# Graph layer on one core: attention columns copied by VectorE, SiLU on ScalarE, four groups gathered ahead

## The chip, the cores and the metric

The kernel runs on one core of one Trainium2 chip. The metric is the device time of one execution in microseconds, as a median over several executions; lower is better. The engines are called by the profile's names: PE (TensorE), DVE (VectorE), ACT (ScalarE), POOL (GpSimd) and SP (SyncE, which issues most DMAs).

## The reference

A graph layer with attention over 12,500 nodes of 64 features and 412,500 edges, sorted by receiver (`dst`); `src` is random.

```python
h = jnp.maximum(_layernorm(x, axis=-1), 0.0)
msg_in = jnp.concatenate([h[src], h[dst], edge_attr_32], axis=-1)
messages = swish(msg_in @ W1 + b1) @ W2 + b2
att = softmax(swish(msg_in @ Wa1 + ba1) @ Wa2 + ba2, axis=0)   # over all edges
agg = segment_sum(messages * att, dst)
out = x + swish(concat([h, agg]) @ Wu1 + bu1) @ Wu2 + bu2
```

## The kernel before, in words

**The head.** Nodes are padded to 12,544 and worked in seven chunks: layer norm on DVE and ACT, a transpose on PE into `hT` (features by nodes, kept in SBUF), then two tables in DRAM: `ts_d`, one row of 128 numbers per node for its part as sender, and `tr_d`, the same as receiver. All weights of the first products are halved, so that a SiLU is made as (tanh(y) + 1) y with y half the argument.

**The groups.** The edges lie in 403 groups of K = 8 tiles of 128 edges. `one_pass` is one unrolled loop over the groups g; `pin` keeps the written order on each engine. For each group:

- `load(g)`, two groups ahead: POOL gathers the sender rows from `ts_d` by one indirect DMA for each tile (L513) into a buffer `gs` of a pool of seven; SP loads receiver windows of `tr_d` into `wins`; DVE makes a 0/1 matrix `eo` (L538); PE multiplies both into the PSUM tile `pe` (L542), which holds the receiver and edge parts of 1,024 edges.
- `begin(g)`: DVE adds the gathered rows to `pe` (L553), ACT takes the tanh (L556).
- `end(g)`: DVE makes the messages (L566), the attention activation (L572), multiplies by `Wa2` (L574) and reduces to logits (L577).
- `weigh(s)`, once for each batch of four groups: the running maximum (L603, L604, L606), two exponentials on ACT (L607, L610).
- `by_node(g)`, four to five groups later: DVE makes for each of the eight tiles a matrix `wt` of weight where receiver equals column (L620), PE multiplies it with the messages (L626), ACT copies the sum (L632), PE projects it (L637), and `put(g)` adds it to the node table `sums` (L651, L655) and notes the maximum in `stand` (L658), at columns held in registers.

**Columns.** For every second group from 8 on (`picks`, 192 groups, one tile each) no row is gathered for the eighth tile. Instead ACT copies the 128 senders' columns of `hT` one by one into a tile `cols` (L483: 128 partitions by 4 bytes, the column in a register), DVE blanks the wrong half (L547), and PE multiplies with the sender weights into `pe` (L548). `spots` holds the columns' places; a register load (L479, `TENSOR_LOAD` in the trace) puts 32 of them at a time into ACT's registers, before 32 copies (`columns`, `burst`). Register loads for `put` and for the windows are at L498.

**The tail.** After the last group the node update runs in 13 tiles on all engines.

Of the kernel before, what the change touches and what calls it, by code (L numbers as in the profile page):

```python
# [39 lines left out]
PHASE = 0  # L40
FIRST = 8
SLOTS = (((0, 32), (32, 32)), ((64, 32), (96, 32)))
HT_AT = 4224
ROUND = 12582912.0
WIDE = 128
EPS = 1e-5
# [11 lines left out]
def gnn_kernel(ctx: ExitStack, tc: tile.TileContext, n_edges, x, src, src_row, dst, dst_row, first, edge,  # L58
# [73 lines left out]
    with tc.tile_pool(name="node1", bufs=1) as node1, \  # L132
# [3 lines left out]

        sizes = [8] + [min(CB, NB - 16 - c) for c in range(0, NB - 16, CB)] + [8] if NB > 16 else [NB]
# [38 lines left out]
        pin(nc.scalar.activation(node1.tile([P, 1], F32, name="spare"), eps, AF.Sqrt))  # L176
        xms, sqs, rstds, hs, tss = ({} for _ in range(5))
# [5 lines left out]
        def subtract(i):  # L183

            n = chunks[i][1]
            total = node.tile([P, CB], F32, name="total")[:, :n]
            pin(nc.vector.tensor_reduce(total, xcs[i], AX.X, ALU.add))
            xm = xms[i] = node.tile([P, CB, D], F32, name="xm", bufs=3)[:, :n, :]
            pin(nc.vector.scalar_tensor_tensor(xm, total[:, :, None].to_broadcast([P, n, D]), -1.0 / D,
                                               xcs[i], op0=ALU.mult, op1=ALU.add))  # L190

        def square(i):
            n = chunks[i][1]
            sq = sqs[i] = node.tile([P, CB, D], F32, name="sq", bufs=3)[:, :n, :]
            pin(nc.scalar.activation(sq, xms[i], AF.Square))

        def totals(i):
            n = chunks[i][1]
            rstd = rstds[i] = node.tile([P, CB], F32, name="rstd")[:, :n]
            pin(nc.vector.tensor_reduce(rstd, sqs.pop(i), AX.X, ALU.add))  # L200
# [4 lines left out]
        def normal(i):  # L205
            n = chunks[i][1]
# [37 lines left out]
        nch = len(chunks)  # L244
# [22 lines left out]
        for c, nn in chunks:  # L267
# [9 lines left out]
            pin(nc.sync.dma_start(  # L277
                tr_d[:NP, :].rearrange("(p b) f -> p b f", b=NB)[:, c:c + nn, :], tr))
        pin(nc.sync.dma_start(tr_d[NP:, :], zero[:WR, :]))
# [80 lines left out]
def one_pass(tc, n_edges, v):  # L360
# [17 lines left out]
    with ExitStack() as ctx:  # L378
# [43 lines left out]
        with tc.tile_pool(name="work2", bufs=2) as work2, \  # L422
                tc.tile_pool(name="small", bufs=3) as small, \
                tc.tile_pool(name="pre_ps", bufs=AHEAD + 1, space=PSUM) as pre_ps, \
                tc.tile_pool(name="one_ps", bufs=1, space=PSUM) as one_ps:
            pes, gss, lgs, ps_, psums, sps, pps, ees, mts, nums, cols = ({} for _ in range(11))
# [12 lines left out]
            chosen = {g: i for i, g in enumerate(picks)}  # L439
            hT8 = v["hT"].rearrange("d b p -> d (b p)").bitcast(U8)  # L440
            sets = [(i, min(P, len(picks) - i)) for i in range(0, len(picks), P)]
# [3 lines left out]
            def places():  # L445
# [4 lines left out]
                for k, (i, n) in enumerate(sets):  # L450
                    e = (picks[i] * K + K - 1) * EP
                    nc.sync.dma_start(num[:n, k, :], bass.AP(
                        tensor=v["src_row"].tensor, offset=v["src_row"][:, e:].offset,
                        ap=[[EVERY * K * EP, n], [1, EP]]))
# [8 lines left out]
                for k, (i, n) in enumerate(sets):  # L463
                    nc.sync.dma_start(par_d[k * P:k * P + n, :], low[:n, k, :])
# [3 lines left out]
            def numbers(g):  # L468
                if g in chosen:
                    n = nums[g] = small.tile([P, EP], I32, name="half", bufs=3)  # L470
                    row = par_d[chosen[g]:chosen[g] + 1, :]
                    nc.sync.dma_start(n, bass.AP(tensor=row.tensor, offset=row.offset, ap=[[0, P], [1, EP]]))
                    cols[g] = small.tile([P, EP], F32, name="cols", bufs=3)

            def columns(g, first, n):
                if g not in chosen:
                    return
                to, i = cols[g].bitcast(U8), chosen[g]
                _, regs = nc.values_load_multi_w_load_instructions(  # L479
                    spots[i % P:i % P + 1, i // P, first:first + n], engines=[ENG.Activation],  # L480
                    min_val=HT_AT, max_val=HT_AT + 2 * NP - 4, skip_runtime_bounds_check_because=WHY)
                for i in range(n):
                    pin(nc.scalar.copy(to[:, 4 * (first + i):4 * (first + i) + 4],  # L483
                                       hT8[:, bass.ds(regs[i] - HT_AT, 4)]))

            def burst(g, k):
# [6 lines left out]
            tr_w = bass.AP(tensor=tr_d.tensor, offset=tr_d.offset,  # L493
                           ap=[[C, NP + WR - SHIFT], [SHIFT * C, 2], [1, C]])

            def registers(g, engine, at, base=base_sb, top=NP - 1):
                n = min(NQ, NG + (base is not base_sb) - g)
# [6 lines left out]
            def load(g):  # L504

                t = g * K
                if g % NQ == 0:
                    registers(g, ENG.SP, at_sp)
                full = gather.tile([P, K, C], F32, name="gs")
                gs = gss[g] = full[:EP]  # L510
                for j in range(K - (g in chosen)):
# [21 lines left out]
                for r in range(2):  # L533
                    nc.sync.dma_start(win[r * R:(r + 1) * R, :, r, :],
                                      tr_w[bass.ds(at_sp[g], R), :, :])
# [14 lines left out]
            def begin(g):  # L550

                n = K - (g in chosen)
                pin(nc.vector.tensor_tensor(gss[g][:, :n, :], pes[g][:, :n, :], gss[g][:, :n, :], ALU.add))  # L553
                if n < K:
                    pin(nc.vector.tensor_copy(gss[g][:, n, :], pes[g][:, n, :]))
                pin(nc.scalar.activation(pes[g], gss[g], AF.Tanh))  # L556

            def end(g, then=None):

                s = batch[g]  # L560
                if g == starts[s]:
                    lgs[s] = small.tile([EP, B * K], F32, name="lg")
                gs, th = gss.pop(g), pes.pop(g)

                def message():
                    pin(nc.vector.scalar_tensor_tensor(acts[g % ACTS][:, :, 0:U], th[:, :, U:C], 1.0,  # L566
                                                       gs[:, :, U:C], op0=ALU.add, op1=ALU.mult))

                if g < NG - 1:
                    message()  # L570
                att = th[:, :, 0:U]
                pin(nc.vector.scalar_tensor_tensor(att, th[:, :, 0:U], 1.0, gs[:, :, 0:U],  # L572
                                                   op0=ALU.add, op1=ALU.mult))
# [3 lines left out]
                pin(nc.vector.tensor_reduce(lgs[s][:, k:k + K], att, AX.X, ALU.add))  # L577
# [4 lines left out]
                if g == NG - 1:  # L582
                    message()

            def top(s):

                n = size[s] * K
                lg = lgs[s]
# [10 lines left out]
            def weigh(s):  # L599
# [5 lines left out]
                fall = small.tile([P, 1], F32, name="fall")  # L605
                pin(nc.vector.tensor_tensor(fall, nmax[:, s + 1:s + 2], nmax[:, s:s + 1], ALU.subtract))  # L606
# [3 lines left out]
                pin(nc.scalar.activation(p[:, :n], lgs.pop(s)[:, :n], AF.Exp, bias=nmax[:EP, s + 1:s + 2],  # L610
                                         accum_out=psum))
                psums[s] = psum

            def by_node(g):
# [4 lines left out]
                for j in range(K):  # L619
                    pin(nc.vector.tensor_scalar(wt[:, j, :], iota_w[:EP, j // H, :],  # L620
                                                dloc[:, g * K + j:g * K + j + 1],
                                                p[:, k + j:k + j + 1],
                                                op0=ALU.is_equal, op1=ALU.mult))
# [94 lines left out]
            for g in range(NG):  # L718
# [6 lines left out]
                begin(g)  # L725
                if more and g < NG - 1:
# [10 lines left out]
                if g + AHEAD < NG:  # L737
                    load(g + AHEAD)
                numbers(g + 6)
# [384 lines left out]
```

## Time and profile before

| | |
|---|---|
| median of 3 runs | 3902.49 us (3900.42 to 3908.46) |
| the profiled execution's own time | 3904.89 us |
| its span, first to last instruction | 3903.1 us |
| busy PE, DVE, ACT, POOL | 61%, 80%, 76%, 74% of the span |

A row of the grouped view reads: line, engine, operation, written tile <- read tiles, shapes, count, then busy time in us, mean of one in ns, then idle time of the engine just before these instructions and what ended it. "issue" is idle time for which the profile shows nothing that was waited for. Register loads, waits and DMA issues are work of an engine's sequencer and do not count as busy. An engine runs its instructions in order.

### The profile page before, as it was taken

How to read it: one execution, taken by the hardware profiler on the slowest of the kernel's cores; microseconds unless marked ns; L12 is line 12 of the kernel's file. 1: busy time of each engine (PE TensorE's matmuls, PEld its weight loads, DVE VectorE, ACT ScalarE, POOL GpSimd, SP SyncE). 2: the span in 40 equal slices, each digit the busy share in tenths (PEclk: the TensorE clock that was granted, in tenths of full speed). 3: DMA queues.
4: the chain of work that ended last, by engine and by line, in shares of the span. 5: the costliest groups of instructions: out<-in, count | busy, mean ns of one | idle time of the engine just before them, and what ended most of it. 6: DMA issues, size and time to landing. Idle time of an engine off the chain costs nothing. (4 is left out here: it accounts for less than half of the span.)

```text
span 3903.1 us, 72226 instructions
## 1 busy us (share of the span) xinstructions
PE 2368.6 (61%) x11368; PEld 1927.2 (49%) x11368; DVE 3115.4 (80%) x8929; ACT 2954.1 (76%) x25797; POOL 2888.6 (74%) x3057
## 2 busy tenths in 40 slices
PE   6566656666666666665665656556565565555655
PEld 5454444454445554554444545445444454444545
DVE  6888787878788888887877877778777777877887
ACT  2887777777778888887877777878877878878712
POOL 3777777777777777777777777777777777777774
PEclk8766566666666657666666666666666666666666
DMA  7433334333433333333333333333333333333343
GB/s 280 114 104 94 102 100 106 94 104 99 107 93 97 97 97 91 94 97 94 87 97 85 97 93 89 97 86 97 93 88 97 86 96 91 90 97 86 95 116 86
DMA packets 228304, 391.30 MB, mean 100 GB/s; under 512 B 72369, under 2 KB 155762, under 8 KB 214770
## 3 DMA queue, kind: packets, MB, share of 16 engines
q0 software_dynamic: 97024, 198.90, 19.5%
q1 hardware_dynamic: 130802, 187.73, 17.9%
q14 instruction: 385, 3.15, 0.3%
q8 instruction: 93, 1.52, 0.2%
HBM read 360.52 MB, written 25.82 MB: 99 GB/s over the span
## 5 line engine op out<-in xcount | busy, mean ns | idle before, releaser
L513 POOL DMA_INDIRECT gs<-ts_d,src_sb x3032 | 2871.4, 947 | 973.1 <-issue 844.2
L483 ACT COPY cols<-hT 128x4 uint8 x24576 | 2415.5, 189 | 595.2 <-issue 594.2
L542 PE MATMUL pe<-wins,eo 128*128 128x256 f32 x3224 | 1470.7, 630 | 846.4 <-DVE eo L538 619.9
L542 PEld LDWEIGHTS pe<-wins,eo 128*128 128x128 f32 x3224 | 964.4, 316 | 1145.4 <-DVE eo L538 708.6
L620 DVE TENSOR_SCALAR wt<-iota_w,dloc,p 128x40 f32<-128x40 f32 x3224 | 726.9, 323 | 1.8
L553 DVE TENSOR_TENSOR gs<-pe,gs 128x1024 f32<-128x1024 f32 (+1 forms) x403 | 467.0, 1159 | 325.7 <-DMA gs<-ts_d,src_sb 303.3
L626 PE MATMUL sp<-wt,acts 128*65 128x40 f32 x6448 | 621.9, 268 | 4.6 <-DVE wt L620 3.5
L626 PEld LDWEIGHTS sp<-wt,acts 128*65 128x65 f32 x6448 | 586.0, 183 | 11.4 <-DVE wt L620 6.2
L556 ACT ACTIVATE pe<-gs 128x1024 f32<-128x1024 f32 x403 | 410.6, 1019 | 215.9 <-DVE gs L553 125.3
L637 PEld LDWEIGHTS mt<-ss,w2u 65*128 65x128 f32 x806 | 201.7, 281 | 330.4 <-issue 291.9
L637 PE MATMUL mt<-ss,w2u 65*128 65x40 f32 x806 | 183.7, 322 | 255.5 <-DVE gm L603 221.4
L566 DVE SCALAR_TENSOR_TENSOR acts<-pe,gs 128x512 f32<-128x512 f32 x403 | 277.6, 689 | 21.6 <-ACT pe L556 12.2
L574 DVE TENSOR_TENSOR pe<-pe,w_all 128x512 f32<-128x512 f32 x403 | 281.8, 699 | 13.5
L572 DVE SCALAR_TENSOR_TENSOR pe<-pe,gs 128x512 f32<-128x512 f32 x403 | 280.3, 696 | 10.5
L596 PE MATMUL mt<-ident,mx 128*128 128x128 f32 x107 | 46.7, 437 | 396.4 <-DVE sums L655 375.9
L577 DVE TENSOR_REDUCE lg<-pe 128x8 f32<-128x512 f32 x403 | 276.7, 687 | 10.5
L538 DVE TENSOR_SCALAR eo<-dbs,bj 64x256 f32<-64x256 int32 x806 | 275.5, 371 | 9.2
L596 PEld LDWEIGHTS mt<-ident,mx 128*128 128x128 f32 x107 | 19.2, 179 | 408.3 <-issue 404.5
L658 DVE COPY stand<-nmax 64x40 f32 x806 | 159.0, 197 | 3.4 <-issue 0.3
L547 DVE SCALAR_TENSOR_TENSOR cols<-half,cols 128x128 f32<-128x128 int32 x192 | 67.1, 349 | 100.6 <-ACT cols L483 98.5
L651 DVE SCALAR_TENSOR_TENSOR sums<-sums,scale,mt 64x40 f32 x214 | 54.4, 254 | 110.9 <-PE mt L637 107.4
L548 PEld LDWEIGHTS pe<-stack,cols 128*128 128x128 f32 x384 | 121.7, 317 | 32.5
(126 smaller groups left out, 957.6 us busy)
## 6 DMA issues: line engine op xcount, KB each, us to landing
eo<-in_edge_dram SPq DMA_DIRECT2D x100, 512.0 KB
dbs<-in_dst_row_dram SPq DMA_DIRECT2D x200, 256.0 KB
gs<-ts_d,src_sb POOLq DMA_INDIRECT x3032
wins<-tr_d SPq DMA_DIRECT2D x806, 32.0 KB
half<-par_d SPq DMA_DIRECT2D x192, 64.0 KB
ts_d<-ts SPq DMA_DIRECT2D x5, 896.0 KB
tr_d<-tr SPq DMA_DIRECT2D x5, 896.0 KB
hT_d<-hT SPq DMA_DIRECT2D x7, 448.0 KB
```

The lines of the kernel that those rows point to most:

```text
L483: pin(nc.scalar.copy(to[:, 4 * (first + i):4 * (first + i) + 4], hT8[:, bass.ds(regs[i] - HT_AT, 4)]))
L513: nc.gpsimd.indirect_dma_start(out=full[:rows, j, :], out_offset=None, in_=ts_d[:, :], in_offset=bass.IndirectOffsetOnAxis(ap=src_full[:ro ...
L542: pin(nc.tensor.matmul(pe[:, 2 * q:2 * q + 2, :], eo[:, q * EP:(q + 1) * EP], win[:, q // 2, :, :], start=True, stop=q < H - 1 or g not in ...
L553: pin(nc.vector.tensor_tensor(gss[g][:, :n, :], pes[g][:, :n, :], gss[g][:, :n, :], ALU.add))
L556: pin(nc.scalar.activation(pes[g], gss[g], AF.Tanh))
L566: pin(nc.vector.scalar_tensor_tensor(acts[g % ACTS][:, :, 0:U], th[:, :, U:C], 1.0, gs[:, :, U:C], op0=ALU.add, op1=ALU.mult))
L572: pin(nc.vector.scalar_tensor_tensor(att, th[:, :, 0:U], 1.0, gs[:, :, 0:U], op0=ALU.add, op1=ALU.mult))
L574: pin(nc.vector.tensor_tensor(att, att, wa2[:EP, None, :].to_broadcast([EP, K, U]), ALU.mult))
L577: pin(nc.vector.tensor_reduce(lgs[s][:, k:k + K], att, AX.X, ALU.add))
L620: pin(nc.vector.tensor_scalar(wt[:, j, :], iota_w[:EP, j // H, :], dloc[:, g * K + j:g * K + j + 1], p[:, k + j:k + j + 1], op0=ALU.is_equ ...
L626: pin(nc.tensor.matmul(sp, acts[g % ACTS][:, j, :], wt[:, j, :], start=j == 0, stop=j == K - 1))
L637: pin(nc.tensor.matmul(pp, w2u.rearrange("s h u -> s (h u)"), sps.pop(g), start=True, stop=True))
```

## The change

- **Columns move to DVE.** `PHASE = 9` leaves `picks` empty, so ACT copies no column. `vpicks` takes three groups in eight, from 9 to 390: 144 groups, one tile each. In each of the 384 iterations from 4 to 387, `vcolumns` loads 24 registers of DVE twice (after `begin`, and ahead of `end`), and `spare_columns` issues the 24 copies that belong to each load on DVE. In the built program there are 18,432 such copies and 864 loads (96 loads are cut in two where a tile ends). `fetch`, single rows fetched by SP, is off (`ROW0 = 1000`).
- **SiLU on ACT.** `begin` adds into `pe` and ACT makes two SiLUs of 512 elements, attention part and messages; the tanh and the two products on DVE go. `gs` is free after the add.
- **Softmax without Exp.** `weigh` makes exp(x) as ((1 + t) / (1 - t)) to the 16th, t = tanh(x / 32): a tanh and a square on ACT and nine small operations on DVE.
- **`wt` in two operations** of 320 elements in place of eight of 40.
- **Four groups in the head.** Rows of `x` of the first `FILL = 4` groups' senders (32 gathers) are gathered while `ts_d` does not yet exist; the layer norm and the product follow (`filled`), between the pieces of the `tr_d` loop. `load` gathers nothing for these groups.
- SP's window addresses are counted in bytes, so that no multiplication of a register is needed.

```diff
-PHASE = 0
+PHASE = 9
+FILL = 4
+ROW0 = 1000
+VTURN = 8
+VRES = (1, 4, 6)
+VSTART = 4
+VLATER = 5
...
+        early = node1.tile([P, FILL * K], I32, name="early")
+        nc.sync.dma_start(early, src[:, :FILL * K])
+        for g in range(FILL):
+            for j in range(K):
+                nc.gpsimd.indirect_dma_start(out=xes[g][:, j, :], ..., in_=x[:, :], ...)
...
+            def vcolumns(g, part):
+                at, end = (i * EP * len(VRES) // (2 * VTURN) for i in (2 * (g - VSTART) + part, ...
+                while 0 <= at < end:
+                    t, first = vpicks[at // EP], at % EP
+                    n = min(end - at, EP - first)
...
+                    loads, regs = spots_of(t, first, n, ENG.DVE)
+                    to = cols[t].bitcast(U8)
+                    waiting.extend((to[:, 4 * (first + i):4 * (first + i) + 4], regs[i]) for i in range(n))
+                    at += n
+
+            def spare_columns(n=None):
+                for to, reg in waiting[:n]:
+                    pin(nc.vector.tensor_copy(to, hT8[:, bass.ds(reg - HT_AT, 4)]))
...
-                for j in range(K - (g in chosen)):
+                for j in range(K - (g in chosen) - (g in fetched) if g >= FILL else 0):
...
-                pin(nc.vector.tensor_tensor(gss[g][:, :n, :], pes[g][:, :n, :], gss[g][:, :n, :], ALU.add))
-                if n < K:
-                    pin(nc.vector.tensor_copy(gss[g][:, n, :], pes[g][:, n, :]))
-                pin(nc.scalar.activation(pes[g], gss[g], AF.Tanh))
+                pin(nc.vector.tensor_tensor(pe[:, :n, :], pe[:, :n, :], gs[:, :n, :], ALU.add))
+                pin(nc.scalar.activation(att, pe[:, :, 0:U], AF.Silu, scale=2.0))
+                pin(nc.scalar.activation(acts[g % ACTS][:, :, 0:U], pe[:, :, U:C], AF.Silu, scale=2.0))
...
-                    pin(nc.vector.scalar_tensor_tensor(acts[g % ACTS][:, :, 0:U], th[:, :, U:C], 1.0,
-                                                       gs[:, :, U:C], op0=ALU.add, op1=ALU.mult))
-                pin(nc.vector.scalar_tensor_tensor(att, th[:, :, 0:U], 1.0, gs[:, :, 0:U],
-                                                   op0=ALU.add, op1=ALU.mult))
...
-                pin(nc.scalar.activation(scale[:, s:s + 1], fall, AF.Exp))
+                pin(nc.scalar.activation(t, lg[:, :n + 1], AF.Tanh, bias=part, scale=1.0 / 32))
+                spare_columns()
+                pin(nc.vector.tensor_scalar(d, t, -1.0, 1.0, op0=ALU.mult, op1=ALU.add))
+                pin(nc.vector.reciprocal(d, d))
+                pin(nc.vector.scalar_tensor_tensor(t, t, 1.0, d, op0=ALU.add, op1=ALU.mult))
+                for _ in range(3):
+                    pin(nc.vector.tensor_tensor(t, t, t, ALU.mult))
...
-                for j in range(K):
-                    pin(nc.vector.tensor_scalar(wt[:, j, :], iota_w[:EP, j // H, :], ...
+                pin(nc.vector.tensor_tensor(wt.rearrange("p (r h) w -> p r h w", h=H), ..., ALU.is_equal))
+                pin(nc.vector.tensor_tensor(wt, wt, p[:, k:k + K, None].to_broadcast([EP, K, W]), ALU.mult))
...
                 begin(g)
+                vcolumns(g, 0)
...
+                spare_columns()
+                vcolumns(g, 1)
                 end(g)
...
+                spare_columns()
```

More of the change, by code (lines that the diff above doesn't have):

```diff
@@ L242, in senders, with filled @@
                     ts_d.rearrange("(p b) f -> p b f", b=NB)[:, c:c + nn, :], tss.pop(i)))
-        nch = len(chunks)
+        ready = []
+        def filled(i):
+            h = hs.pop(i)
+            pt = node_ps.tile([P, 4, P], F32, name="pt")
+            for k in range(K // 2):
+                pin(nc.tensor.transpose(pt[:, k, :], h[:, 2 * k:2 * k + 2, :], ident))
+            he = node.tile([2 * D, K // 2, P], F32, name="he")
+            pin(nc.scalar.copy(he, pt))
+            gs = gather.tile([P, K, C], F32, name="gs")
+            for b in range(0, K, 4):
+                pn = node_ps.tile([P, 4, C], F32, name="pn", bufs=4)
+                for k in range(0, 4, 2):
+                    pin(nc.tensor.matmul(pn[:, k:k + 2, :], he[:, (b + k) // 2, :],
+                                         w_pair[:, 0], start=True, stop=True))
+                pin(nc.scalar.copy(gs[:, b:b + 4, :], pn))
+            ready.append(gs)
         squares(0)
@@ L278, in gnn_kernel @@
                 tr_d[:NP, :].rearrange("(p b) f -> p b f", b=NB)[:, c:c + nn, :], tr))
+        squares(nch)
+        for i in range(FILL):
+            totals(nch + i)
+            deviation(nch + i)
+            if i + 1 < FILL:
+                subtract(nch + i + 1)
+                square(nch + i + 1)
+            if i > 0:
+                filled(nch + i - 1)
+            for c in chunks[i * nch // FILL:(i + 1) * nch // FILL]:
+                receivers(*c)
+            normal(nch + i)
+        filled(nch + FILL - 1)
         pin(nc.sync.dma_start(tr_d[NP:, :], zero[:WR, :]))
@@ L425, in one_pass @@
                 tc.tile_pool(name="one_ps", bufs=1, space=PSUM) as one_ps:
-            pes, gss, lgs, ps_, psums, sps, pps, ees, mts, nums, cols = ({} for _ in range(11))
+            pes, gss, atts, lgs, ps_, psums, sps, pps, ees, mts, nums, cols = ({} for _ in range(12))
             w2t_ps = one_ps.tile([P, 4, P], F32, name="mt")[:U, 0, :S1]
@@ L484, in columns @@
                                        hT8[:, bass.ds(regs[i] - HT_AT, 4)]))
+            waiting = []
+            def vcolumns(g, part):
+                at, end = (i * EP * len(VRES) // (2 * VTURN) for i in (2 * (g - VSTART) + part,
+                                                                        2 * (g - VSTART) + part + 1))
+                end = min(end, len(vpicks) * EP)
+                while 0 <= at < end:
+                    t, first = vpicks[at // EP], at % EP
+                    n = min(end - at, EP - first)
+                    if first == 0:
+                        cols[t] = small.tile([P, EP], F32, name="vcols", bufs=VBUFS)
+                    loads, regs = spots_of(t, first, n, ENG.DVE)
+                    for one in loads:
+                        pin(one)
+                    to = cols[t].bitcast(U8)
[4 more added lines that the diff above has]
+                    pin(nc.vector.tensor_copy(to, hT8[:, bass.ds(reg - HT_AT, 4)]))
+                waiting[:] = waiting[len(waiting) if n is None else n:]
             def burst(g, k):
@@ L488, in burst @@
                     columns(g + 3 + i, *SLOTS[EVERY - 1 - i][k])
-            at_sp, at_lo, at_hi, bus, rest = {}, {}, {}, {}, {}
[L493 to L497, printed above, removed]
+            fetched = {}
+            for i in range(NG):
+                g = ROW0 + (EP * (i + 1) - 1) // ROWS + 2
+                if g < NG - 12:
+                    fetched[g] = i
@@ new lines, in one_pass, with ask, scaled @@
+            order = list(fetched)
+            ids, lone = {}, {}
+            ts8 = ts_d.rearrange("n f -> (n f)").bitcast(U8)
+            def ask(i):
+                if i < len(order):
+                    g = order[i]
+                    e = (g * K + K - 1 - (g in chosen)) * EP
+                    ids[i] = small.tile([1, EP], I32, name="ids", bufs=2)
+                    nc.sync.dma_start(ids[i], v["src_row"][:, e:e + EP])
+            def scaled(i):
+                if i < len(order):
+                    pin(nc.vector.tensor_scalar(ids[i], ids[i], 9, None, op0=ALU.logical_shift_left))
@@ new lines, in fetch @@
+            def fetch(g):
+                at = (g - ROW0) * ROWS
+                end = min(at + ROWS, len(order) * EP)
+                if g == ROW0 - 3:
+                    ask(0)
+                if g == ROW0 - 2:
+                    scaled(0)
+                while 0 <= at < end:
+                    i, first = at // EP, at % EP
+                    n = min(end - at, EP - first)
+                    if first < ROWS:
+                        ask(i + 1)
+                    if EP // 2 <= first < EP // 2 + ROWS:
+                        scaled(i + 1)
+                    if first == 0:
+                        lone[order[i]] = small.tile([P, C], F32, name="lone", bufs=2)
+                    to = lone[order[i]]
+                    loads, regs = nc.values_load_multi_w_load_instructions(
+                        ids[i][0:1, first:first + n], engines=[ENG.SP], min_val=0, max_val=(NP - 1) * 4 * C,
+                        skip_runtime_bounds_check_because=WHY)
+                    for one in loads:
+                        pin(one)
+                    for k in range(n):
+                        pin(nc.sync.dma_start(to[first + k:first + k + 1, :].bitcast(U8),
+                                          ts8[bass.ds(regs[k], 4 * C)][None, :]))
+                    at += n
@@ new lines, in one_pass, with registers @@
+            at_sp, at_lo, at_hi, bus, rest = {}, {}, {}, {}, {}
+            row = 4 * C
+            tr8 = tr_d.bitcast(U8)
+            tr_w = bass.AP(tensor=tr8.tensor, offset=tr8.offset,
+                           ap=[[1, (NP - 1) * row + 1], [row, R], [SHIFT * row, 2], [1, row]])
+            base_by = keep.tile([1, NG + 1], I32, name="base_by")
+            nc.vector.tensor_scalar(base_by[:, :NG], base_sb[:, :NG], 9, None, op0=ALU.logical_shift_left)
+            def registers(g, engine, at, base, top):
+                n = min(NQ, NG + (base is not base_by) - g)
@@ L738, in one_pass @@
                     load(g + AHEAD)
+                fetch(g)
                 numbers(g + 6)
```

113 lines of the change are left out of this document (69 added, 44 removed).

## The prediction

> **What bounds the kernel now.** I read the busy table, the waits, the costliest groups (different shapes kept apart), and then POOL's timeline at both ends.
>
> ```profile
> PE 2368.6 (61%) x11368; PEld 1927.2 (49%) x11368; DVE 3115.4 (80%) x8929; ACT 2954.1 (76%) x25797; POOL 2888.6 (74%) x3057
> POOL gs L513 <- issue: 844.2, 2770, 0.3
> POOL gs L513 <- DMA ts_d<-ts: 49.3, 1, 49.3
> POOL gs L513 <- DMA gs<-ts_d,src_sb: 34.8, 114, 0.3
> DVE gs L553 <- DMA gs<-ts_d,src_sb: 303.3, 225, 3.9
> L513 POOL DMA_INDIRECT gs<-ts_d,src_sb x3032 | 2871.4, 947 | 973.1 <-issue 844.2 <-DMA ts_d<-ts 49.3 <-DMA gs<-ts_d,src_sb 34.8
> 51.68 1.10 POOL L513 DMA_INDIRECT gs<-ts_d,src_sb  x1 [49.29 <-DMA ts_d<-ts]
> 3845.97 0.94 POOL L513 DMA_INDIRECT gs<-ts_d,src_sb  x1 [0.30 <-issue]
> ```
>
> POOL is only 74% busy, yet after the head no wait of its gathers is longer than 0.3 us, and that gap follows every gather: 0.947 busy, 0.30 between. So POOL is full: (3846.9 - 51.7) / 3032 = 1.2517 us for one gather. The time is 51.7 until `ts_d` exists, 3795 of gathers and 56.2 of tail; 3903.1 in all, and the execution's own time is 1.8 more (3904.9), 2.4 above the median. DVE waits for gathers (303 us), not the reverse. Fewer gathers save, until another engine's group exceeds POOL's.
>
> **POOL after the change.** 192 gathers replaced by ACT's columns become 144 replaced by DVE's, and 32 move to the head: 3224 - 144 - 32 = 3048, sixteen more than 3032. The 32 take 40 us of the 49.3 in which POOL idles, so they are hidden, if their indices land like the first inputs; one small DMA ahead of those on SP costs 0 to 0.6 us. POOL alone would give 51.7 + 3048 x 1.2517 + 56.2 = 3923 us; for one group with its 7.63 gathers, 9.55 us. That is the floor. The question is DVE.
>
> **DVE, ordinary work.**
>
> ```profile
> L620 DVE TENSOR_SCALAR wt<-iota_w,dloc,p 128x40 f32<-128x40 f32 x3224 | 726.9, 323 | 1.8
> L574 DVE TENSOR_TENSOR pe<-pe,w_all 128x512 f32<-128x512 f32 x403 | 281.8, 699 | 13.5
> L572 DVE SCALAR_TENSOR_TENSOR pe<-pe,gs 128x512 f32<-128x512 f32 x403 | 280.3, 696 | 10.5
> L566 DVE SCALAR_TENSOR_TENSOR acts<-pe,gs 128x512 f32<-128x512 f32 x403 | 277.6, 689 | 21.6 <-ACT pe L556 12.2
> L553 DVE TENSOR_TENSOR gs<-pe,gs 128x1024 f32<-128x1024 f32 x211 | 258.0, 1223 | 180.4 <-DMA gs<-ts_d,src_sb 161.4 <-issue 14.9 <-PE pe L542 3.0
> L553 DVE TENSOR_TENSOR gs<-pe,gs 128x896 f32<-128x896 f32 x192 | 209.0, 1089 | 145.3 <-DMA gs<-ts_d,src_sb 141.9 <-issue 0.2
> L555 DVE COPY gs<-pe 128x128 f32<-128x128 f32 x192 | 53.9, 281 | 0.0
> L606 DVE TENSOR_TENSOR fall<-nmax 128x1 f32<-128x1 f32 x107 | 17.0, 159 | 3.7
> L589 DVE TENSOR_TENSOR lg<-lg,w_all 128x32 f32<-128x32 f32 x98 | 18.9, 193 | 3.3
> 3842.18 0.16 DVE L604 TENSOR_TENSOR nmax<-gm,nmax 128x1 f32<-128x1 f32 x1
> 3842.37 0.16 DVE L606 TENSOR_TENSOR fall<-nmax 128x1 f32<-128x1 f32 x1
> 96.00:3850.00 3754.00, 2275.16 (x10973) 1848.37 (x10972) 3012.68 (x8702) 2906.84 (x25703) 2837.77 (x2997) 0.64 0.37 96
> ```
>
> The last row is the busy time of the stretch of all groups (PE, its weight loads, DVE, ACT, POOL): DVE 3012.7. Removed: `wt` 726.9, the two products 277.6 + 280.3, the copy 53.9, `fall` 17.0: 1356. Added: two `wt` operations of 320 elements; on the line from 193 ns for 32 to 699 for 512 each takes 0.50, less the overlap of their end with what follows 0.94 for both: 403 x 0.94 = 379. And nine small operations of a softmax step, each waiting for the one before (L604 and L606 of 0.16 start 0.19 apart), so 0.22 each: 107 x 2.0 = 212. Left are 2248 / 403 = **5.58 us** a group. A step's own wait for ACT's tanh is filled by 24 copies. ACT keeps two SiLUs (at 689 to 1019 ns per 512 to 1024 elements some 1.3 us a group) and is no bound.
>
> **DVE, the copies.** 48 a group, a form DVE does not run before.
>
> ```profile
> L483 ACT COPY cols<-hT 128x4 uint8 x24576 | 2415.5, 189 | 595.2 <-issue 594.2
> 2002.42 0.18 DVE L655 TENSOR_TENSOR sums<-sums,mt 64x40 f32 x1
> 2002.52 0.17 DVE L658 COPY stand<-nmax 64x40 f32 x1
> 2004.89 3.14 ACT L483 COPY cols<-hT 128x4 uint8 x32 [0.28 <-issue]
> 2008.96 3.14 ACT L483 COPY cols<-hT 128x4 uint8 x32 [0.93 <-issue]
> ```
>
> Short operations overlap: what counts is start to start. On ACT it is (3.14 - 0.19) / 31 = 0.095 us. On DVE two operations of 40 elements, both at columns from registers, start 0.10 apart; an element takes (1223 - 1089) / 128 = 1.05 ns (the two shapes of L553), so with 4 elements 0.10 - 0.038 = 0.062. I take 0.07, near DVE's own row, and keep 0.062 to 0.095: 48 x 0.07 = **3.36 us**. [...]
>
> **DVE, the register loads.** They do not count as busy and are the hidden term.
>
> ```profile
> L479 ACTq TENSOR_LOAD <-spots x768: 1942/2008/2800, 98.4 to 3706.6; - x192
> L553 DVEq EVENT_SEMAPHORE  x1420: 21/50/3717, 92.0 to 3849.7; - x178
> L498 DVEq TENSOR_LOAD <-bases x202: 336/343/600, 142.4 to 3853.0; - x101
> L498 SPq TENSOR_LOAD <-base_sb x101: 294/301/753, 87.2 to 3774.6; - x101
> L282 DVEq TENSOR_LOAD <-wrong x1: 321/321/321, 3896.2 to 3896.2; - x1
> L556 ACT ACTIVATE pe<-gs 128x1024 f32<-128x1024 f32 x403 | 410.6, 1019 | 215.9 <-DVE gs L553 125.3 <-DVE gs L555 62.8 <-DMA gs<-ts_d,src_sb 19.5
> ACT cols L483 <- issue: 594.2, 764, 1.3
> DVE sums L651 <- PE mt L637: 107.4, 89, 1.6
> DVE bu L323 <- PE mt L314: 102.8, 25, 4.5
> ```
>
> ACT's load of 32 registers takes 2.008 us. While it runs the sequencer issues nothing; the engine only finishes what is queued. The timeline shows both cases: 0.28 idle where a tanh of 1.02 stood in the queue, 0.93 where only copies did. So 2.01 - 0.93 = 1.08 us of copies were queued, some eleven.
>
> For 24 registers on DVE: SP takes 0.30 for four, ACT 2.008 for 32, so 0.061 for each further one, and 24 need 1.52; DVE's four take 0.343, 1.14 times SP's, which makes 1.74. I take 1.65. The low end is DVE's own slope from one register (0.321) to four (0.343), 0.007 each: 0.49.
>
> In the built order one load stands behind `begin`'s add in three groups of four, behind the second `wt` operation in the fourth, and one behind the first 24 copies in every group. Queued behind it is all of DVE's next work: `put`, `eo`, and the attention product, for which PE and ACT then wait. Cover by queued copies is 11 x 0.07 = 0.8; behind the add it is the add, 1.1, and what the add's split waits leave of the copies (four of 0.05 with as much between them, 0.4). Idle for four groups: three times 0.2 behind the add, 1.2 behind `wt`, four times 0.85 behind copies, 0.3 for a load cut in two, 0.2 for the two loads of `put` (0.343 each): 5.7, or **1.43 us** a group.
>
> **The sum.** 5.58 + 3.36 + 1.43 = 10.37 us a group, above POOL's 9.55: DVE becomes the bound, and POOL waits for `gs`. DVE's chain begins with the first add:
>
> ```profile
> 96.40 1.23 DVE L553 TENSOR_TENSOR gs<-pe,gs 128x1024 f32<-128x1024 f32 x1 [2.96 <-PE pe L542]
> 3849.81 1.23 DVE L553 TENSOR_TENSOR gs<-pe,gs 128x1024 f32<-128x1024 f32 x1 [1.64 <-DMA gs<-ts_d,src_sb]
> ```
>
> In the head DVE has four layer norms more, each four operations of 512 elements (0.7) and a reciprocal: 12 us. They stand among the `tr_d` work, which partly waits for DMAs, so the add at 96.4 comes 0 to 12 later, say 8: 104. (POOL does not feel it at once: groups 0 to 3 are there and three buffers are free.) PE's and ACT's part of these groups lies in ACT's idle stretch before its first tanh. Three sets of `spots` in place of two, and one table load more in the tail, are 1 us each, within that choice. Then 384 x 10.37 = 3982; nineteen groups without copies at 8, between the 5.6 and POOL's 9.98 for eight gathers: 152; from the last add to the end 53 as now. Waits on PE that POOL's pace hid come on top: `bu` 103 in full, `sums` half of 107. Together 104 + 3982 + 152 + 53 + 156 = 4447 us span, with + 1.8 and - 2.4 much the same: **4450 us**. Hidden at no cost: the gathers saved (POOL has 0.82 us a group to spare), the shorter `wt` on PE, SP's addresses. With copies of 0.062 it falls by 147, with loads of 1.52 by 100, without the waits by 156; with loads of 1.74 it rises by 70, with copies of 0.08 by 184.
>
> **The rivals.**
>
> *Loads are cheap on DVE.* With 0.49 us all are covered by queued work. DVE needs 5.58 + 3.36 and the 0.4 of the waits on PE, 9.34 us, below 9.55, and POOL stays the bound: 3923 + 2 = 3925. For it: DVE's flat slope. Against: ACT's 2.008. 11 in 100.
>
> *Gathers get shorter and nothing slows.* The eight `wt` operations ran beside them; without, the mean of 947 falls to the usual 940, and one takes 1.245. Then 51.7 + 3048 x 1.245 + 56.2 = 3903: no slower than now. It decides only if DVE also stays under 9.5. The rows speak against much:
>
> ```profile
> 2000.89 0.94 POOL L513 DMA_INDIRECT gs<-ts_d,src_sb  x1 [0.31 <-issue]
> 2003.91 1.78 DVE L620 TENSOR_SCALAR wt<-iota_w,dloc,p 128x40 f32<-128x40 f32 x8
> 2004.64 0.95 POOL L513 DMA_INDIRECT gs<-ts_d,src_sb  x1 [0.30 <-issue]
> ```
>
> A gather inside the eight takes 0.95, one outside 0.94. 5 in 100.
>
> *The copies block POOL.* If a gather stood still while copies run (3.36 of 9.55 us, 35% of the time), its 0.94 became 1.27, and 3048 x 1.58 + 108 = 4924. By the two rows above the price is 0.01 instead of 0.33; it would decide from 0.12 on, where POOL exceeds 10.37 a group (1.36 x 7.63). 2 in 100. [...]
>
> *No load is covered.* 864 x 1.65 = 1426 us idle in place of 384 x 1.43 = 549: 5325. ACT's 0.28 against 0.93 says cover works. 2 in 100.
>
> That the columns are not made by DVE at all is excluded by the built order.
>
> **How the numbers follow.** 80 in 100 for the forecast, 4450, its own range 4060 to 4750. The whole range reaches down to the cheap loads: 3920 to 4750; outside lie the shorter gathers, blocking, no cover, and the forecast's ends, some 17 in 100. About 0.2% (8 us) is what a measurement here can tell. Of the five for shorter gathers one is for a tail shorter by a product (0.7) and half a `wt` (0.9) at each of its last groups, and so for faster. Faster 0.01, same 0.04, slower 0.95.
>
> **What would show it.** Right: POOL's gathers waiting for DVE's add, not in 0.3 us steps; DVE register loads of 24 near 1.65 us; copies of 0.07 start to start; DVE idle by "issue" of some 500 us in front of copies, products and `sums`; ACT busy below 25%. Wrong: gathers still end to end at 1.25 us in mid-span (then 3925), or loads under 1 us.

## The result, and the profile after

The changed kernel takes 4679.15 us (median of 4 runs, 4676.97 to 4682.63) against 3901.9 (3900.42 to 3908.46): ratio 1.1989, 95% interval 1.1968 to 1.201. It is slower by 777 us; 4450 was forecast, with a range of 3920 to 4750. The profiled execution's own time is 4678.03, its span 4676.3.

The page's busy line, the groups and the waits of the kernel after:

```profile
PE 2366.9 (51%) x11320; PEld 1939.5 (41%) x11320; DVE 3762.2 (80%) x24774; ACT 603.4 (13%) x1645; POOL 2982.4 (64%) x3105
L649 POOL DMA_INDIRECT gs<-ts_d,src_sb x3048 | 2928.1, 961 | 1617.3 <-issue 791.5 <-DVE pe L690 752.3 <-DVE near L517 32.1
L568 DVE COPY vcols<-hT 128x4 uint8 x18432 | 1423.3, 189 | 119.3 <-issue 118.9
L706 DVE TENSOR_TENSOR att<-att,w_all 128x512 f32<-128x512 f32 x403 | 278.8, 692 | 375.3 <-issue 374.0 <-ACT att L695 1.2
L798 DVE TENSOR_TENSOR sums<-sums,mt 64x40 f32 x592 | 114.7, 194 | 110.9 <-issue 98.4 <-PE mt L780 0.4
L766 DVE TENSOR_TENSOR wt<-wt,p 128x320 f32<-128x320 f32 x403 | 199.3, 494 | 13.9
POOL gs L649 <- DVE pe L690: 752.3, 351, 7.5
DVE bu L377 <- PE mt L368: 105.9, 25, 4.5
DVE sums L794 <- issue: 24.5, 80, 0.7
DVE pe L690 <- issue: 7.8, 33, 0.6
```

POOL, which before never waited longer than 0.3 us in mid-span, now waits 351 times for DVE's add to give a buffer back, 752 us in all. DVE is no busier by its share than before (80%), but it has become the bound: of what it waits for, little but `bu` is late in mid-span, for 106 us in all, much as before. The rest of its idle time is mostly put down to "issue", in front of the product L706, the copies and `sums`. That is where its sequencer loads registers:

```profile
L535 DVEq TENSOR_LOAD <-spots x864: 592/1610/1961, 131.8 to 4506.5; - x173
2102.54 0.49 DVE L766 TENSOR_TENSOR wt<-wt,p 128x320 f32<-128x320 f32 x1
2102.95 1.80 DVE L568 COPY vcols<-hT 128x4 uint8 x24
2105.66 0.69 DVE L706 TENSOR_TENSOR att<-att,w_all 128x512 f32<-128x512 f32 x1 [0.91 <-issue]
2106.39 0.69 DVE L709 TENSOR_REDUCE lg<-att 128x8 f32<-128x512 f32 x1
2106.99 1.82 DVE L568 COPY vcols<-hT 128x4 uint8 x24
2108.84 1.23 DVE L690 TENSOR_TENSOR pe<-pe,gs 128x1024 f32<-128x1024 f32 x1
2110.22 0.19 DVE L798 TENSOR_TENSOR sums<-sums,mt 64x40 f32 x1
```

The first row is the loads' durations (lowest, median, highest, in ns); the others are DVE's timeline. Behind the first 24 copies comes a load (here 1.64 us, from 2103.93 on). The last copies run out while it lasts, and the product starts 0.91 us late. Then the next 24 copies run without a gap ahead of them.

The stretches of the span, from the adds L690 of the first five and of the last fifteen groups, and the busy time between them (PE, weight loads, DVE, ACT, POOL):

```profile
L690 DVE TENSOR_TENSOR pe<-pe,gs x5: 1222/1223/1233, 115.5 to 130.9; 128x1024 f32<-128x1024 f32 x5
L690 DVE TENSOR_TENSOR pe<-pe,gs x15: 1099/1232/1233, 4511.9 to 4622.1; 128x1024 f32<-128x1024 f32 x13, 128x896 f32<-128x896 f32 x2
130.90:4511.90 4381.00, 2174.36 (x10397) 1780.87 (x10396) 3540.72 (x24198) 506.27 (x1439) 2831.10 (x2950) 0.61 0.32 78
```

So 115.5 of head, 15.4 and 110.2 for the groups without copies, 4381 for the 384 iterations with copies (11.41 each, DVE 9.22 busy and 2.19 idle) and 54.2 of tail.

### The profile page after: what moved, and what is told of

Its sections match the earlier page's. It is cut to its first block, busy times and chain, and to the rows that moved or that the text cites. A ratio compares the mean times of both kernels' runs of the same rounds, so it can differ in the third digit from the quotient of the medians.

```text
span 4676.3 us, 61394 instructions
## 1 busy us (share of the span) xinstructions
PE 2366.9 (51%) x11320; PEld 1939.5 (41%) x11320; DVE 3762.2 (80%) x24774; ACT 603.4 (13%) x1645; POOL 2982.4 (64%) x3105
## 5 line engine op out<-in xcount | busy, mean ns | idle before, releaser
L649 POOL DMA_INDIRECT gs<-ts_d,src_sb x3048 | 2928.1, 961 | 1617.3 <-issue 791.5
L568 DVE COPY vcols<-hT 128x4 uint8 x18432 | 1423.3, 189 | 119.3 <-issue 118.9
L695 ACT ACTIVATE att<-pe 128x512 f32<-128x512 f32 x403 | 240.7, 597 | 3042.6 <-DVE pe L690 3042.5
L706 DVE TENSOR_TENSOR att<-att,w_all 128x512 f32<-128x512 f32 x403 | 278.8, 692 | 375.3 <-issue 374.0
L690 DVE TENSOR_TENSOR pe<-pe,gs 128x1024 f32<-128x1024 f32 (+1 forms) x403 | 475.9, 1181 | 31.0 <-issue 7.8
L709 DVE TENSOR_REDUCE lg<-att 128x8 f32<-128x512 f32 x403 | 274.9, 682 | 10.6 <-issue 0.2
L696 ACT ACTIVATE acts<-pe 128x512 f32<-128x512 f32 x403 | 238.7, 592 | 0.0
L766 DVE TENSOR_TENSOR wt<-wt,p 128x320 f32<-128x320 f32 x403 | 199.3, 494 | 13.9
L798 DVE TENSOR_TENSOR sums<-sums,mt 64x40 f32 x592 | 114.7, 194 | 110.9 <-issue 98.4
L763 DVE TENSOR_TENSOR wt<-iota_w,dloc 128x320 f32<-128x320 f32 x403 | 199.4, 495 | 1.6
L740 ACT ACTIVATE t<-lg,part 128x33 f32<-128x33 f32 (+2 forms) x107 | 34.5, 322 | 642.0 <-DVE part L738 642.0
```

Source lines behind the costliest of these rows:

```text
L568: pin(nc.vector.tensor_copy(to, hT8[:, bass.ds(reg - HT_AT, 4)]))
L649: nc.gpsimd.indirect_dma_start(out=full[:rows, j, :], out_offset=None, in_=ts_d[:, :], in_offset=bass.IndirectOffsetOnAxis(ap=src_full[:ro ...
L690: pin(nc.vector.tensor_tensor(pe[:, :n, :], pe[:, :n, :], gs[:, :n, :], ALU.add))
L695: pin(nc.scalar.activation(att, pe[:, :, 0:U], AF.Silu, scale=2.0))
L696: pin(nc.scalar.activation(acts[g % ACTS][:, :, 0:U], pe[:, :, U:C], AF.Silu, scale=2.0))
L706: pin(nc.vector.tensor_tensor(att, att, wa2[:EP, None, :].to_broadcast([EP, K, U]), ALU.mult))
```

## The experiments

The theory to be tested: DVE's queue is the bound, by copies and by register loads for which too little is queued. The rivals: something else of the change sets the pace (POOL's gathers, the SiLU on ACT, the softmax chain), or the loads' idle time is only where another wait shows. The kernel before ran again beside each group of tests. It took 3900.81 and 3902.42 us beside those whose times are compared here, against 3901.9 beside the change; only the last group differs.

### The loads taken away

Copies from fixed columns: the same 18,432 copies, not of the senders that the edges name, and no register load for them.

```diff
-                    loads, regs = spots_of(t, first, n, ENG.DVE)
-                    for one in loads:
-                        pin(one)
...
-                    pin(nc.vector.tensor_copy(to, hT8[:, bass.ds(reg - HT_AT, 4)]))
+                    pin(nc.vector.tensor_copy(to, hT8[:, reg % (2 * NP - 4):reg % (2 * NP - 4) + 4]))
```

> After, with the 18,432 copies from fixed columns and without the 864 register loads; left out is which column is copied. Theory: the load idle of 1.66 us a group goes, DVE needs 11.41 - 1.66 = 9.75 us a group, just above POOL's 9.55: about 4040 us. If an address from a register also slows a copy, down to POOL's floor, 54.7 + 3815 + 55 = 3925 us. Rival (the copies are the cost and the loads were hidden): above 4500 us.

Measured 4100.11 us, 1.0512 times before (1.0481 to 1.0542). Groups of this kernel:

```profile
L646 POOL DMA_INDIRECT gs<-ts_d,src_sb x3048 | 2965.7, 973 | 1028.3 <-issue 836.6 <-DVE pe L687 70.8 <-DVE near L517 35.1
L565 DVE COPY vcols<-hT 128x4 uint8<-128x4 uint8 x18432 | 1421.0, 193 | 0.0
```

The copies cost what they cost before (1421 against 1423), have no idle time ahead of them, and the kernel is 579 us faster than the change. The loads are the largest part of the loss. POOL waits for DVE for only 71 us and is the bound again, yet at 4100 rather than 4040: its gathers take 973 ns in place of 947, 79 us in all. The row's 35.1 us are one more cost: POOL has gathered three groups by 84.8 us and then stands until DVE's first add gives a buffer back, at 119.6 (`near` is what DVE runs just behind that add).

### One load moved under the product

The second load of each iteration is issued behind the attention product, so that the reduce and not the product stands behind it; the copies stay where they were.

```diff
                 pin(nc.vector.tensor_tensor(att, att, wa2[:EP, None, :].to_broadcast([EP, K, U]), ALU.mult))
+                if g < NG - 1:
+                    vcolumns(g, 1)
...
-                vcolumns(g, 1)
                 end(g)
```

> After, with the second register load of each group moved behind DVE's attention product instead of ahead of it; the same instructions otherwise. Theory (the load stalls DVE as far as no queued work covers it): ten copies and the product of 0.69 cover 1.4 of 1.61 us, the 374 us of idle time before the product shrink to some 90 before the reduction behind it: about 4390 us. Rival (the idle time before the product is a wait for ACT's SiLU or for something else that the profile calls issue): 4679 us, the idle time stays where it was.

Measured 4383.97, 1.1239 (1.1207 to 1.1272), 6 us from the theory. The rows:

```profile
L706 DVE TENSOR_TENSOR att<-att,w_all 128x512 f32<-128x512 f32 x403 | 273.9, 680 | 1.2 <-ACT att L695 1.2
L711 DVE TENSOR_REDUCE lg<-att 128x8 f32<-128x512 f32 x403 | 276.4, 686 | 167.6 <-DVE att L706 163.7 <-issue 3.3
POOL gs L649 <- DVE pe L690: 390.0, 224, 6.7
```

The 374 us ahead of the product are gone, 164 come back ahead of the reduce, and POOL's wait for DVE falls from 752 to 390. The same work in the same number of instructions is 295 us faster. Here a load's price was its length less what was queued on the engine when it started: 0.97 us of idle time behind copies alone (374.0 / 384), 0.43 behind copies and the product (163.7 / 384). That the time came so close is in part luck. Some 90 us of idle time were expected ahead of the reduce and 164 came; 30 us less ahead of `sums` L794 and 44 us less busy time, which nothing here explains, made up for it.

### Two columns in eight groups, and none

The number of columns alone. With two groups in eight, 96 tiles are still made of columns (`VLATER`, which sets the first of them, goes from 5 to 6); with none, every tile is gathered.

```diff
-VRES = (1, 4, 6)
+VRES = (2, 6)
```

> Two groups in eight instead of three: 32 copies a group, loads of 16 registers. Theory: DVE needs 5.5 busy and 0.5 of small waits, 2.5 of copies and 0.65 of load idle, 9.2 us a group, below POOL's 9.70 with 3096 gathers, so POOL bounds: 54.7 + 3875 + 55 = 3985 us, no waits of POOL for DVE's add. Rival (each column costs the same wherever DVE stands, a straight line between none and three): 4488 us.

```diff
-VRES = (1, 4, 6)
+VRES = ()
```

> The change with no columns at all: the 144 tiles are gathered again, everything else as after. Theory (DVE's copies and register loads set the time): DVE falls to some 6.0 us a group, POOL's 3192 gathers at 1.2517 us bound it again: 54.7 + 3995 + 55 = 4105 us, 570 less than after although POOL has 144 gathers more. Rival (SiLU on ACT, the longer softmax or the two wt operations slow the loop): 4300 us or more, with POOL still waiting for DVE.

Measured 4118.99 with two (1.056; 1.0529 to 1.0591) and 4229.38 with none (1.0843; 1.0811 to 1.0874). Both miss the theory, by 134 and 124 us. With two, the rival's 4488 is far off. With none, 4229 lies nearer to the rival's 4300 than to the theory's 4105; what speaks against the rival is that POOL hardly waits for DVE. POOL's gathers of the two:

```profile
L649 POOL DMA_INDIRECT gs<-ts_d,src_sb x3096 | 3019.0, 975 | 989.6 <-issue 872.0 <-DVE pe L690 45.1 <-DVE vcols L568 26.8
```

```profile
L650 POOL DMA_INDIRECT gs<-ts_d,src_sb x3192 | 3113.4, 975 | 1007.9 <-issue 940.8 <-DVE eo L675 33.4 <-DMA gs<-ts_d,src_sb 23.2
```

POOL is the bound in both, as the theory has it: its one long wait for DVE is that for the first add (34.5 and 33.1 us). But a gather takes 975 ns, not 947. Without columns that is 3113.4 - 3192 x 0.947 = 91 us, and with the 33 of the first wait it is the miss of 124. Something else of the change lengthens gathers, and not the copies, for there are none.

### What lengthens the gathers

The timeline without columns shows it at one place:

```profile
2000.30 0.94 POOL L650 DMA_INDIRECT gs<-ts_d,src_sb  x1 [0.30 <-issue]
2001.39 0.49 DVE L767 TENSOR_TENSOR wt<-wt,p 128x320 f32<-128x320 f32 x1
2001.54 1.15 POOL L650 DMA_INDIRECT gs<-ts_d,src_sb  x1 [0.30 <-issue]
2001.79 0.69 DVE L707 TENSOR_TENSOR att<-att,w_all 128x512 f32<-128x512 f32 x1
2003.00 0.94 POOL L650 DMA_INDIRECT gs<-ts_d,src_sb  x1 [0.30 <-issue]
```

The gather that starts inside the second `wt` product takes 1.15 us, its neighbours 0.94. Counted over the trace: of the 2388 gathers with neither `wt` product (L764, L767) nor the attention product (L707) beside them 0.1% take over 1 us. The 804 others hold the rest, 100 us beyond 944 ns each. These three DVE operations read both operands from SBUF; the kernel before had none of the three (its `wt` had one tensor operand, its product read PSUM). The loss depends on when the gather starts. 251 gathers start inside an attention product. The 218 that do so in its first 0.35 us all end 0.81 to 0.83 us behind the product's end, whenever they began; the 33 later ones take their usual 943 ns. So in this trace the product holds the gathers that start early in it until it is over.

The test leaves the attention SiLU in PSUM, in the tile `pe`, so that the product reads one operand from each memory. There are no columns here either.

```diff
-                att = atts[g] = silus.tile([P, K, U], F32, name="att")[:EP]
+                att = atts[g] = pe[:, :, 0:U]
```

> The kernel after, without any column (every one of the 3224 tiles gathers both terms in the head or by its own gather) and with the attention copy of the silu left in PSUM, so that DVE's attention product reads one operand from PSUM instead of two from SBUF. Theory (a DVE product with both operands in SBUF lengthens the gather beside it): the two products of wt still have both operands in SBUF, so part of the lengthening stays; 3192 gathers x 1.252 = 3996, head 52, tail 57, and 15 ns a gather for what stays (the gathers of the same program had a mean of 958 ns in the trace where they had 975 without the move): 48. 4153 us, 4130 to 4180. Rival (the operands' memory does not matter): 4229 again, as the same kernel with the copy in SBUF.

Measured 4160.63, 1.0663 (1.0645 to 1.068), 69 us less than with the copy in SBUF.

```profile
L650 POOL DMA_INDIRECT gs<-ts_d,src_sb x3192 | 3043.7, 954 | 1007.4 <-issue 940.5 <-DVE eo L675 30.1 <-DMA gs<-ts_d,src_sb 24.4
2002.93 0.70 DVE L707 TENSOR_TENSOR pe<-pe,w_all 128x512 f32<-128x512 f32 x1
2003.03 0.94 POOL L650 DMA_INDIRECT gs<-ts_d,src_sb  x1 [0.30 <-issue]
```

The gathers' sum falls by 3113.4 - 3043.7 = 70 us, and the time by as much. That the place of the attention copy costs this is shown: none of the 242 gathers that now start inside the product takes over 948 ns. Three other things moved with the copy. Without columns and with the copy in SBUF, gathers that start inside the SiLU L696, which wrote it there, have a mean of 946 ns, and those inside the reduce, which read it there, 943. In the kernel before, none of the 216 that start inside the messages' product L566, which writes into SBUF and reads one operand from there, takes over 957. By this elimination it is the second SBUF operand; no test changes that operand alone. What stays lies beside the two `wt` products (29 us beyond 944 ns). That 4153 came within 8 us is in part luck: beyond 947 ns each the gathers hold 21 us and not 48, and the first wait for DVE, 30 us, was left out.

### Columns back on ScalarE: no better version

If POOL sets the time once DVE is relieved, the columns can go back to ACT, with the rest of the change kept and the copy in PSUM, and DVE can make a few more.

```diff
-PHASE = 9
+PHASE = 0
...
-VRES = (1, 4, 6)
+VRES = ()
```

> The kernel after with all columns moved back to ScalarE (half of the groups, 192 columns as before the change), none on VectorE, and the attention copy in PSUM; the head's early gathers, the two silus on ScalarE and the two products for wt stay as the change made them. Theory (GpSimd's gathers set the time once DVE's columns are gone): 3000 gathers, 32 fewer than before, 3903 - 32 x 1.252 = 3863, and 15 ns a gather for the products of wt, 45: 3908 us, 3880 to 3930. Rival (ScalarE's two silus behind its column copies delay DVE's add and so GpSimd): 3950 or more, with GpSimd waiting for DVE's add in the list of waits.

> As the version with the columns on ScalarE, and every eighth group a column on VectorE besides, with its second register load issued behind the attention product: 2953 gathers. Theory (GpSimd sets the time): 3908 - 47 x 1.252 = 3849 us, 3820 to 3880. Rival (ScalarE's or VectorE's queue sets it): 3903 or more.

> As the version before it, with two VectorE columns in eight groups. Theory (GpSimd sets the time as long as DVE's work of a group is shorter than GpSimd's): about 2907 gathers, 3849 - 46 x 1.252 = 3791 us if DVE keeps up; DVE's group is 5.5 of ordinary work, 12 copies x 0.071 = 0.85 in the mean, and two loads of 12 registers of some 0.85, of which the second is covered, with 0.4 of waits: 7.6 to 8.5, under GpSimd's 9.0. 3791 us, 3770 to 3850. Rival (DVE is the bound again): 3900 or more, with GpSimd waiting for DVE's add for over 200 us.

The second and the third have `VRES = (7,)` and `(3, 7)`, `VLATER` set to fit, and the load moved as above. Measured 4423.31 (1.1336; 1.1317 to 1.1355), 4448.86 (1.1397; 1.1378 to 1.1416) and 4483.14 (1.1485; 1.1466 to 1.1504). The theory fell in all three, and all passed the rivals' marks. The first of them:

```profile
PE 2384.2 (54%) x11416; PEld 1878.6 (42%) x11416; DVE 2365.7 (54%) x6390; ACT 3010.4 (68%) x26221; POOL 2937.9 (66%) x3057
L546 ACT COPY cols<-hT 128x4 uint8 x24576 | 2425.3, 190 | 923.4 <-issue 919.9 <-DMA dbs<-in_dst_row_dram 2.6
L684 DVE SCALAR_TENSOR_TENSOR cols<-half,cols 128x128 f32<-128x128 int32 x192 | 67.4, 351 | 653.9 <-ACT cols L546 653.5
L743 DVE TENSOR_SCALAR d<-t 128x33 f32<-128x33 f32 (+2 forms) x107 | 19.6, 183 | 647.8 <-ACT t L741 647.8
L707 DVE TENSOR_TENSOR pe<-pe,w_all 128x512 f32<-128x512 f32 x403 | 281.7, 699 | 423.3 <-ACT acts L697 416.3
POOL gs L650 <- DVE pe L691: 491.1, 117, 8.0
```

ACT is busy or stalled at a load for 3010 + 923 = 3934 us, where before it was 2954 + 595 = 3549. The 24,576 copies are the same; the loads cost 920 in place of 594, and the two SiLUs take 0.58 and 0.60 us where the one tanh before took 1.02. DVE now waits for ACT at three places, 1718 us in all (columns, tanh, SiLU), and POOL behind it. With the bound there, the columns added on DVE saved gathers that nobody waited for: 47 and 95 fewer, and 26 and 60 us more. Which of the two moves, the SiLUs or the tanh of the softmax, does the harm was not separated.

### A group on another chip

The kernels of three of these tests, and the change with the attention copy in PSUM, had run once before.

> The version without columns, with one thing changed: ACT's SiLU of the attention part stays in PSUM (in place in pe), so that DVE's product with Wa2 has one input in SBUF instead of two. In the version without columns POOL's gathers average 975 ns where before they took 947; those beside this product average 1144, those beside PSUM-reading operations 944. Theory (a DVE operation with two SBUF inputs holds up POOL's gather): some 435 gathers lose 0.2 us, 87 us: 4229 - 87 = 4142 us, mean of a gather near 948. Rival (the gathers are longer for another reason, as more of them in flight or the DMA queue): 4229 us, mean 975.

> Columns back on ACT for every second group as before, none on DVE; SiLU on ACT, softmax without Exp, wt in two operations and four groups in the head stay; attention part in PSUM. POOL gathers 3224 - 192 - 32 = 3000. Theory (POOL bounds, ACT still has room): 52 + 3000 x 1.258 + 55 = 3881 us, 0.5% below before. Rival (two SiLUs of 0.6 us in place of one tanh of 1.02, beside 64 copies and two register loads of 2.0 us a group, make ACT the bound): 3950 us or more, POOL waiting for DVE's add, which waits for nothing of ACT but later products do.

> The same with columns on both engines: ACT every second group, DVE one group in eight (48 more), the second load behind the product, loads of 8 registers. POOL gathers 2952. Theory (DVE at some 7.7 us a group has room, POOL at 9.2 bounds): 52 + 2952 x 1.258 + 55 = 3821 us, 2% below before. Rival (ACT, at some 9 us a group, bounds): 3880 us, no gain over columns on ACT alone.

> After, with the attention part in PSUM and nothing else changed. Theory (in after DVE bounds, POOL waits 750 us for it, and longer gathers cost nothing): within 15 us of 4679. Rival (the longer gathers are part of what after lost): 4600 us or less.

On the chip of that group the kernel before itself took 5978.91 us. Measured there: 5515.96 without columns (0.9235 of before; 0.9176 to 0.9294), 6286.32 with columns on ACT (1.0525; 1.0459 to 1.059), 6406.62 with one on DVE besides (1.0726; 1.0652 to 1.08), and 5444.99 for the change with the copy in PSUM (0.9116; 0.9064 to 0.9168). The wait row of the columns on ACT there:

```profile
ACT cols L546 <- issue: 2351.1, 3092, 1.8
```

ACT stood idle ahead of a copy 3092 times with no cause that the profile shows, against 767 times for the same program on the other chip. Without columns the idle time lies elsewhere: 2964 us ahead of ACT's copy `ss`, ended by what the profile calls "remote", where the same program on the other chip has none, and POOL waits for DVE's add for 1280. What slows that chip is open, and the group decides none of the claims, so the first three were repeated. It shows that the order of the kernels can turn over with the chip: the kernel without columns and with the copy in PSUM is faster than before there (0.92) and slower on the other chip (1.07). What the PSUM copy alone does to the changed kernel stays open; the changed kernel itself did not run on that chip.

## Why the prediction was right, and where it was off

- **POOL full before, DVE the bound after: right.** POOL's waits for DVE's add are the row it named (752 us), and taking away the loads or columns gives the bound back to POOL.
- **Head: 104 forecast, 115.5 measured.** The first add comes 19 us later than in the kernel before, not 0 to 12: DVE now also waits for PE among the `tr_d` work, 6.6, 5.8 and 3.8 us between the pieces of the four layer norms. The tail was forecast at 53 and is 54.2, the groups without copies at 152 and are 125.6.
- **DVE's ordinary work: 5.58 a group forecast.** (3540.72 - 1423.3) / 384 = 5.51. Right.
- **The copies: 3.36 forecast, 3.71 measured; +133 us.** The step that failed is the count of a burst as 24 starts: start to start is 0.070 ((1.80 - 0.19) / 23, from the timeline) as taken, but a burst ends with a whole copy of 0.19, so 1.80 and not 1.68; the mean of all bursts is 1423.3 / 768 = 1.85. So 92 of the 133 us are the ends, and the rest are bursts slower than the one shown. The 77 ns of busy time a copy (1423.3 / 18432) contain the burst's end.
- **The register load: 1.65 us forecast, 1.63 measured** (median of the 672 loads of 24 registers; the row's 1.61 is that of all 864). The halves of the cut loads take 0.61 for 8 registers and 1.11 for 16, so the slope from SP and ACT was right, and DVE's own slope from one to four registers misled the rival of cheap loads.
- **Idle for loads: 1.43 a group forecast; 1.62 measured.** The rows above give 374.0 + 118.9 + 98.4, and two of 24.5 and 7.8 for `sums` L794 and the add: 624 us, 75 more. Behind 24 copies 0.85 was forecast; 0.91 stands in the timeline, and the mean is 374.0 / 384 = 0.97.
- **Waits and small gaps: 0.41 a group forecast, 0.56 measured.** The wait for `bu` is 106 as said, that for `sums` nearly gone (0.4). In its place are gaps of 10 to 14 us in a line, like the 13.9 ahead of L766, which the sum left out: idle 840 in all, less 624 and the 106 of `bu`, leaves 110.
- **Together** 11.41 against 10.78 a group: 243 us, of which 133 copies, 135 idle time, less 25 of ordinary work; with 11 in the head and 26 less at the groups without copies it is the 229 between the forecast span 4447 and 4676. The mechanism held; what was too small is the size of two terms, the copies and the idle time, and they err the same way.
- **POOL's floor: wrong, and hidden.** "9.55 us a group" took the gathers as unchanged and DVE's later first add as free. With fixed columns, which has as many gathers, they take 79 us more and POOL waits 35 for that add, so the floor was some 114 us higher, near 4040. It did not matter, because DVE stayed above it; the rival of cheap loads, at 3925, would have missed by that much. The rival of shorter gathers had the sign wrong: it weighed eight operations taken away and not that the two put in their place, and the product, read two operands from SBUF; without columns the gathers beside these three hold 100 us beyond 944 ns each.
- **Copies that block POOL: rightly small.** In the changed kernel the 1304 gathers beside column copies, and beside none of the three products, have a mean of 945 ns; those beside neither have 944.

## What to carry to other kernels

A register load stalled DVE by its length less what was queued ahead of it (0.97 us behind copies, 0.43 behind copies and the product), so put it behind the longest operation, and price it by the number of registers (0.61 us for 8, 1.63 for 24). Before moving work to an engine, lay its idle time beside its busy time, and count a burst with its last instruction's end (24 copies took 1.80 us, not 24 x 0.07 = 1.68). When a bound moves back to GpSimd's gathers, look at which VectorE operations beside them read two operands from SBUF (gathers that started inside one took 1126 ns in the mean, not 944), and at when their buffers come free for the first time (33 to 35 us of waiting here).

## What the runs showed of the hardware

- An indirect gather of 128 rows took 944 ns beside none of the three DVE products of two SBUF operands and up to 1.46 us when it started inside one: without columns, 62% of the 479 gathers that did so are over 1 us, with a mean of 1126 ns. A held gather ended 0.81 to 0.83 us behind the end of the attention product.
- A load of 8 registers took 0.61 us on DVE, of 16 1.11 and of 24 1.63, one of 32 on ACT 2.01. While it ran, the engine went on only with what it had queued: behind 24 copies DVE then stood idle for 0.97 us in the mean.
- The same programs took 1.33 to 1.53 times as long on one chip as on another (5516 against 4161 without columns and with the copy in PSUM, 5979 against 3902 for the kernel before), so that a ratio holds for its chip. Why is open.
